# The last batch's down product in seven half-size products, with its norms taken in halves of columns

## The chip, the cores and the metric

The kernel runs on one core of one Trainium2 chip. The metric is the device time of one execution in microseconds (us); the profile's span, from the first to the last instruction, is about 1 to 2 us shorter. Engines in the profile: PE (TensorE, matrix products), PEld (its weight loads), DVE (VectorE), ACT (ScalarE), POOL (GpSimd) and SP (SyncE, which here issues nearly all DMAs). All data are float32; a float32 matmul shows as two records.

## The reference

Eight batches of 512 tokens of width 512 go through an attention block and then a feed-forward block:

```python
x = x + layernorm(attention(layernorm(x)))
x = x + layernorm(ffn(layernorm(x)))
```

The change concerns the end of the second line. In the feed-forward block

```python
x = fwht(x * SU_ug) / SCALE
x_up = x @ W_up.T * (Wscale_ug[:INTER] * SCALE)        # 512 -> 2048 features
x_gate = x @ W_gate.T * (Wscale_ug[INTER:] * SCALE)
x = silu(x_gate) * x_up
x = fwht(x * SU_dp) / SCALE
x = x @ W_down.T * (Wscale_dp * SCALE)                 # 2048 -> 512: the down product
```

the Walsh-Hadamard transform ahead of the down product is linear, so the kernel applies it to the weights once. What is left for each batch is a product of 512 tokens x 2048 features with 2048 x 512 weights, a scale for each output column (`wsdp_bc`, the column scales copied to all partitions), a normalization of each token over its 512 columns (mean, variance, no weights), and the addition of the block's input.

## The kernel before

Attention for all eight batches takes the first 930 us or so. While it runs, the transformed down weights are written to a DRAM tensor, `wdd`. Its output, the feed-forward block's input, goes to the DRAM tensors `x1d[b]`.

The feed-forward block handles the batches in pairs. Up and gate products are made by seven products in place of eight (Strassen's scheme in Winograd's form), two batches being the two halves of the columns. From the second pair on a second level of the same scheme lies inside the first (`deep`, L1113): matmuls `d` of 128x128 weights by 128x256. Their results are summed on DVE (L1133 to L1144) and POOL (L1140, L1142, L1347) into tiles `pr`; ACT applies silu (L1164), and DVE multiplies gate, up and scale into a feature tile `g` (L1160). `g` holds 128 features x 512 tokens and is the stationary operand of the down product.

The down product of batches 0 to 6 (`psy`, L1225) is spread between the `d` matmuls of later batches. For each of the 16 feature tiles, four matmuls, one for each 128 tokens, add into four PSUM banks; the weights `wd` come from DRAM into three buffers in turn (`wd_load`, L1077). Batch b's end (`finish`, L1245) multiplies the banks by the column scales on DVE (L1250), takes the statistics (`bn`, L97: bn_stats, then bn_aggr), the inverse deviation on POOL (`inverse_std`, L102: an add at L104, a power at L105), the shift on DVE (`shift_of`, L108), the normalization on ACT (L1272) and the residual's addition on POOL (L1275), and stores (L1276). The residuals `xres` are loaded two at a time.

The last batch, 7, has nothing to be spread between. Its 16 weight tiles are loaded ahead (`wd_load_last`, L1085), the first eight into two of the tiles `xb` that had held the inputs, the last eight into two tiles `wdl`. After the last `d` matmul of the kernel, `down_rows` (L1514) makes its product `psz` (L1516): 14 of the 16 matmuls of the first 128 tokens, then the 12 matmuls that batch 6 still lacks (three feature tiles by four row blocks), then the other two, and then 16 for each of the other three row blocks. `end_rows` (L1520) ends a row block while the next one is multiplied. Each of its steps is one instruction over 128 tokens x 512 columns. Only that of the fourth row block has no matmuls beside it.

This part of the program is written under a manual schedule: each engine executes its instructions in the order in which the code issues them, with semaphore waits for operands and for the reuse of buffers. So the order of the calls is the order of the queues of PE, DVE, ACT, POOL and SP. Four PSUM banks are handed out in turn by `ubank` (L978); six buffers of 128x2x512 by `pr_tile` (L997).

Of the kernel before, what the change touches and what calls it, by code (L numbers as in the profile page):

```python
# [10 lines left out]
F32 = mybir.dt.float32  # L11
BF16 = mybir.dt.bfloat16
I32 = mybir.dt.int32
AF = mybir.ActivationFunctionType
ALU = mybir.AluOpType
AX = mybir.AxisListType

P = 128
# [3 lines left out]
NT = S // P  # L22
INTER = 2048
NI = INTER // P
# [9 lines left out]
def sandwich_kernel(  # L34
# [19 lines left out]
    nc = tc.nc  # L54
# [6 lines left out]
    stat = ctx.enter_context(tc.tile_pool(name="stat", bufs=12))  # L61
# [13 lines left out]
    wsdp_bc = const.tile([P, D], F32, name="wsdp_bc")  # L75
# [21 lines left out]
    def bn(dst, src, name):  # L97
        st = stat.tile([P, 6], F32, tag="st", name=f"st_{name}")
        nc.vector.bn_stats(out=st, in_=src)
        nc.vector.bn_aggr(out=dst, in_=st)  # L100

    def inverse_std(mv, n, name):  # L102
        rs = stat.tile([P, NT], F32, tag="rs", name=f"rs_{name}")
        nc.gpsimd.tensor_add(rs[:, :n], mv[:, :n, 1], eps[:, :n])  # L104
        nc.gpsimd.tensor_tensor(rs[:, :n], rs[:, :n], nhalf[:, :n], ALU.pow)  # L105
        return rs

    def shift_of(mv, rs, n, name):  # L108

        sh = stat.tile([P, NT], F32, tag="sh", name=f"sh_{name}")  # L110
        if n == 1:
            nc.vector.tensor_scalar(sh[:, 0:1], mv[:, 0, 0:1], rs[:, 0:1], -1.0, ALU.mult, ALU.mult)
            return sh
        nc.vector.scalar_tensor_tensor(
            sh[:, :n], mv[:, :n, 0], -1.0, rs[:, :n], ALU.mult, ALU.mult
        )
        return sh
# [4 lines left out]
    NH = NI // 2  # L122
# [31 lines left out]
    rows = [(b, t) for b in range(NB) for t in range(NT)]  # L154
    room = {}
    xrow, xflat, xb = {}, {}, {}
# [63 lines left out]
    ops, home = {}, []  # L220
# [21 lines left out]
    with ExitStack() as actx:  # L242
# [474 lines left out]
        for t in range(NT):  # L717
            xn[0, t] = row.tile([P, D], F32, tag="xn", name=f"xn_0_{t}", bufs=3)
            rs, sh = norm0[t]
# [139 lines left out]
        for t in range(NG * NT):  # L859
            n, c = divmod(t, NT)  # L860
            b, i = divmod(t, NK * NT)
# [73 lines left out]
        b = NB - 1  # L935
# [24 lines left out]
        for qc in range(NT):  # L960
            y, rs, sh = ys.pop((b, qc))
# [16 lines left out]
    def ubank(name):  # L978
        return ps_u.tile([P, S], F32, tag="u", name=name)
# [8 lines left out]
    HS = S // 2  # L988
# [8 lines left out]
    def pr_tile(name):  # L997
        return fs.tile([P, 2, S], F32, tag="pr", name=name, bufs=6)
# [72 lines left out]
    def order_of(b):  # L1071
        return [f for i in range(NH) for f in ((i, i + NH) if b % 2 == 0 else (i + NH, i))]
# [10 lines left out]
    wd_last = []  # L1083
# [11 lines left out]
    wd_home = []  # L1095
# [53 lines left out]
    waiting = {b: [] for b in range(NB)}  # L1149
# [136 lines left out]
    def proceed(by=None):  # L1286
        if ends and by in (None, ends[0][0]):
            ends.pop(0)[1]()
# [3 lines left out]
    def part():  # L1292
        if not queue:
            queue.extend(down_parts())
        if queue:
            queue.pop(0)()
# [210 lines left out]
        scale(b, f, c[:, 1], c[:, 0])  # L1507


    b = NB - 1  # L1510
    blocks = [g for _, g, _, _ in waiting[b]]
    assert order_of(b) == [f for f, _, _, _ in waiting[b]]

    def down_rows(ps, t, lo, hi):  # L1514
        for n in range(lo, hi):
            nc.tensor.matmul(  # L1516
                ps, lhsT=blocks[n][:, ts(t, P)], rhs=wd_last[n], start=n == 0, stop=n == NI - 1
            )

    def end_rows(ps, t, eng):  # L1520
        y = pr_tile(f"fy_{b}_{t}")[:, 0]
        nc.vector.tensor_mul(y, ps, wsdp_bc)
        mv = stat.tile([P, NT, 2], F32, tag="mvf", name=f"mvz_{t}")
        bn(mv[:, 0, :], y, f"z{t}")
        rs = inverse_std(mv, 1, f"z{t}")
        sh = shift_of(mv, rs, 1, f"z{t}")
        nc.scalar.activation(y, y, AF.Identity, bias=sh[:, 0:1], scale=rs[:, 0:1])
        eng.tensor_add(y, rest[t], y)
        nc.sync.dma_start(out=out[b, ts(t, P), :], in_=y)

    now[0] += 2
    while queue:
        part()
    ps = ubank("psz_0")
    down_rows(ps, 0, 0, NI - 2)
    while turn_of[0] < b:
        down()
    while ends:
        proceed()
    down_rows(ps, 0, NI - 2, NI)  # L1540
    rest = []
    for t in range(NT):
        rest.append(fs.tile([P, D], F32, tag="sig", name=f"xres_{b}_{t}", bufs=4))
        nc.sync.dma_start(out=rest[t], in_=x1d[b][ts(t, P), :])
    for t in range(NT):
        if t + 1 < NT:
            following = ubank(f"psz_{t + 1}")
            down_rows(following, t + 1, 0, NI)
        end_rows(ps, t, nc.vector if t == NT - 1 else nc.gpsimd)
        ps = following  # L1550


def _rope_table():
# [61 lines left out]
```

## Time and profile before

| | us |
|---|---|
| median of three runs (2101.5 to 2102.11) | 2101.69 |
| profiled execution, device time | 2102.66 |
| profiled execution, span | 2100.9 |
| PE busy | 2076.8 (99% of the span) |
| DVE busy | 1414.4 (67%) |
| POOL busy | 1575.4 (75%) |
| ACT busy | 745.3 (35%) |

The stretch that the change touches is the last 73 us. Busy times in four parts of it, from the profile's windows (from:to, length, then busy us and instructions of PE, PEld, DVE, ACT and POOL, the granted clock as a share of full, the DMA share and GB/s):

```profile
2027.80:2039.90 12.10, 12.10 (x30) 5.40 (x29) 3.26 (x3) 0.72 (x1) 5.59 (x5) 1.00 0.75 260
2039.90:2050.10 10.20, 10.20 (x26) 4.46 (x25) 2.05 (x3) 0.00 (x0) 0.00 (x0) 1.00 0.00 0
2050.10:2093.20 43.10, 43.07 (x101) 18.80 (x99) 9.11 (x23) 5.37 (x7) 12.14 (x15) 1.00 0.25 79
2093.20:2100.90 7.70, 0.00 (x0) 0.00 (x0) 2.48 (x5) 0.81 (x1) 0.74 (x2) 0.67 0.09 35
```

The rows are batch 7's first matmuls, batch 6's last twelve, the rest of batch 7, and what follows PE's last matmul. Times in the text are on this axis, from the span's start. In a row of the timeline the columns are start, length, engine, line, operation, output<-input, shape and count, and in brackets the engine's idle time before it with what ended it.

### The profile page before, as it was taken

To read this page: it belongs to the slowest core of one execution; us is meant where nothing else is said; L and a number is where in the kernel's file an instruction comes from. 1 tells how busy PE (TensorE), PEld (TensorE's weight loads), DVE (VectorE), ACT (ScalarE), POOL (GpSimd) and SP (SyncE) were. 2 spreads that over 40 slices of the span, in tenths; PEclk is the share of its full clock that TensorE was granted. 3 is DMA by queue.
4 is the path that set the end of the run, shared out by engine and by line. 5 is a ranking of instruction groups with operands and counts; after the bars stand their busy time and mean duration, and the time that the engine had idled before them with its cause. 6 is when DMAs were issued, how large, how long until landed. Compare 5 with 4: busy or idle time off the path is not lost.

```text
span 2100.9 us, 26741 instructions
## 1 busy us (share of the span) xinstructions
PE 2076.8 (99%) x9035; PEld 1057.4 (50%) x9042; DVE 1414.4 (67%) x2356; ACT 745.3 (35%) x1199; POOL 1575.4 (75%) x1629
## 2 busy tenths in 40 slices
PE   8999999999999999999999999999999999999998
PEld 4333333333333333344444677676676766777753
DVE  5698777676767677465545866678866678656542
ACT  3554545555555545522121122222222222222211
POOL 4787979787878889645453678788888879787852
PEclk9999999999999999999999999999999999999999
DMA  3112121212121122237454444444343344444432
GB/s 122 37 31 51 42 54 49 47 51 52 46 57 46 32 66 72 70 104 221 145 166 152 146 143 148 133 138 149 130 157 131 131 137 144 138 158 136 138 112 70
DMA packets 215913, 218.12 MB, mean 104 GB/s; under 512 B 87376, under 2 KB 147920, under 8 KB 215776
## 3 DMA queue, kind: packets, MB, share of 16 engines
q1 hardware_dynamic: 215424, 215.32, 33.2%
q8 instruction: 72, 1.18, 0.2%
q0 software_dynamic: 352, 1.08, 0.1%
q14 instruction: 65, 0.53, 0.1%
HBM read 169.18 MB, written 46.92 MB: 103 GB/s over the span
## 4 chain that ended last, share of the span: by engine, by line
PE 94%; DVE 3%; issue 1%; POOL 1%; ACT 1%; DMA 0%; SPq 0%; POOLq 0%; DVEq 0%; ACTq 0%
PE d L1123 24%; PE psy L1225 18%; PE s L527 6%; PE ops L606 6%; PE ps_k L439 5%; PE ps_y L662 5%; PE t L573 5%; PE u L1106 5%; PE g L1106 4%; PE psz L1516 3%; PE t L564 3%; PE l L623 2%; PE ps_q L454 2%; PE ps_v L466 1%; PE ps_cq L407 1%; PE fxh L207 1%
## 5 line engine op out<-in xcount | busy, mean ns | idle before, releaser
L1225 PE MATMUL psy<-wd,g 128*128 128x512 f32 x896 | 448.9, 592 | 0.0
L535 DVE TENSOR_REDUCE nm<-s 128x2 f32<-128x1024 f32 x256 | 300.8, 1216 | 175.1 <-PE s L527 175.1
L1347 POOL TENSOR_TENSOR pr<-pr,pr 128x512 f32<-128x512 f32 x294 | 391.6, 1357 | 9.0
L594 POOL TENSOR_TENSOR p<-p,p 128x512 f32<-128x512 f32 x244 | 330.2, 1384 | 22.1 <-PE ops L606 22.1
L585 ACT ACTIVATE p<-t 128x1024 f32<-128x1024 f32 x256 | 251.8, 1023 | 89.0 <-PE t L573 89.0
L1123 PE MATMUL d<-xb,wq 128*128 128x256 f32 x992 | 254.2, 380 | 1.9 <-DVE inner L1139 1.4
L1123 PEld LDWEIGHTS d<-tt,wq 128*128 128x128 f32 x864 | 164.0, 190 | 144.4 <-issue 106.0
L1123 PE MATMUL d<-tt,wq 128*128 128x256 f32 x864 | 233.8, 379 | 0.2 <-DVE pr L1144 0.2
L1140 POOL TENSOR_TENSOR pr<-inner 128x256 f32<-128x256 f32 x168 | 126.0, 750 | 138.5 <-DVE inner L1139 105.9
L1123 PEld LDWEIGHTS d<-xb,wq 128*128 128x128 f32 x992 | 186.7, 190 | 62.4 <-issue 30.1
L1225 PEld LDWEIGHTS psy<-wd,g 128*128 128x128 f32 x896 | 169.7, 190 | 49.3 <-issue 29.4
L1136 ACT COPY inner<-d 128x256 f32<-128x256 f32 x168 | 62.6, 373 | 309.6 <-PE d L1123 291.5
L1132 ACT COPY inner<-d 128x256 f32<-128x256 f32 x168 | 62.6, 372 | 300.3 <-PE d L1123 193.2
L527 PE MATMUL s<-kT,qT 32*128 32x512 f32 x1024 | 153.8, 639 | 0.7 <-DVE nm L535 0.7
L573 PE MATMUL t<-qT,kT 32*128 32x512 f32 x1024 | 142.8, 598 | 0.0
L606 PE MATMUL ops<-p,v 128*32 128x512 f32 x1024 | 136.8, 605 | 0.0
L1142 POOL TENSOR_TENSOR pr<-pr,inner 128x256 f32<-128x256 f32 x168 | 136.5, 813 | 0.0
L1123 PE MATMUL d<-T,wq 128*128 128x256 f32 x496 | 127.6, 380 | 0.2
L1144 DVE TENSOR_TENSOR pr<-d,inner 128x256 f32<-128x256 f32 x168 | 70.5, 420 | 75.5 <-PE d L1123 72.9
L439 PE MATMUL ps_k<-xT,wkr_sb 128*128 128x512 f32 x256 | 118.3, 605 | 0.7 <-ACT xT L397 0.7
L662 PE MATMUL ps_y<-wo_sb,oT 128*128 128x512 f32 x256 | 115.8, 593 | 0.9 <-DVE oT L657 0.6
L1135 DVE TENSOR_TENSOR inner<-d,inner 128x256 f32<-128x256 f32 x168 | 70.5, 419 | 62.4 <-PE d L1123 62.0
(219 smaller groups left out, 3263.8 us busy)
## 6 DMA issues: line engine op xcount, KB each, us to landing
wq<-wdeep SPq DMA_DIRECT2D x168, 448.0 KB, 4.2
wd<-wdd SPq DMA_DIRECT2D x112, 256.0 KB, 2.8
wdeep<-w SPq DMA_DIRECT2D x32, 448.0 KB, 5.5
xr<-in_x SPq DMA_DIRECT2D x32, 256.0 KB, 2.8
xin<-x1d SPq DMA_DIRECT2D x32, 256.0 KB, 4.0
xres<-x1d SPq DMA_DIRECT2D x32, 256.0 KB, 3.3
out<-fy SPq DMA_DIRECT2D x32, 256.0 KB, 2.0
rec<-rd SPq DMA_DIRECT2D x124, 64.0 KB, 2.0
```

The costliest lines, as they stand in the source:

```text
L439: nc.tensor.matmul(ps, lhsT=wkr_sb[:, k, ts(g, P)], rhs=xT[b][:, k, :], start=(k == 0), stop=(k == NK - 1),)
L527: nc.tensor.matmul(sp[j // 2][:, j % 2, :], lhsT=qT[b][rows, g, ts(qc, P)], rhs=kT[b][rows, g, :], start=True, stop=True,)
L535: nc.vector.tensor_reduce(nms[n][:, qc, 2 * h : 2 * h + 2], sp[h], AX.X, ALU.max, negate=True)
L573: nc.tensor.matmul(sp[j // 2][:, j % 2, :], lhsT=kT[b][rows, g, ts(c, P)], rhs=qT[b][rows, g, :], start=False, stop=True,)
L585: nc.scalar.activation(pt[n, c, h], sp[h], AF.Exp)
L594: nc.gpsimd.tensor_add(into, into, pt[n, c, j // 2][:, j % 2, :])
L606: nc.tensor.matmul(o_ps[n][j * DH : (j + 1) * DH, :], lhsT=vv[b][:, c, ds(g * P + j * DH, DH)], rhs=pt[n, c, j // 2][:, j % 2, :], start=( ...
L662: nc.tensor.matmul(ps, lhsT=oT[b][:, k, ts(qc, P)], rhs=wo_sb[:, k, :], start=False, stop=(k == NK - 1),)
L1106: nc.tensor.matmul(ps, lhsT=w[:, SLOT[n], k, :], rhs=rhs[:, k, :], start=k == 0, stop=k == 1)
L1123: nc.tensor.matmul(ps, lhsT=w[:, INNER[m]], rhs=rhs[m], start=True, stop=True)
L1225: nc.tensor.matmul(ys_[t], lhsT=g[:, ts(t, P)], rhs=w, start=n == 0, stop=n == NI - 1)
L1347: nc.gpsimd.tensor_add(pr[n][:, h], pr[a][:, h], pr[b][:, h])
```

## The change

The last batch's down product is cut in two along features (tiles 0 to 7 and 8 to 15), tokens (0 to 255 and 256 to 511) and output columns (0 to 255 and 256 to 511), and made by seven products instead of eight. Each has 8 feature tiles x 2 row blocks = 16 matmuls of 128x128 by 128x256, summed over the features in one PSUM bank that holds both row blocks. In the order 1, 2, 5, 6, 7, 3, 4:

- The operands that are sums of features (`sums_of`) are made on POOL, 8 instructions of 128x256 each for products 5, 6, 7 and 3, and those that are sums of weights on DVE, 4 instructions of 128x512 each for products 5, 6, 7 and 4; product 4's weights are also multiplied by the column scales (8 more of 128x256). The sums for 5, 6 and 7 are issued ahead of batch 6's ending, those for 3 and 4 after it.
- Four matmuls of product 1 stand ahead of batch 6's twelve.
- The results are combined by ACT copies, DVE and POOL additions of whole banks. The column scales are applied to the combined tiles (L1625 to L1627), before product 4 in the code.
- Statistics are taken for half rows (`rows_stats`, L1619) and joined by bn_aggr. The closing steps (`close_rows`, L1629) go over half rows too: DVE multiplies by the inverse deviation and adds the residual in one instruction (L1638), ACT adds the shift (L1639), and SP stores half rows (L1640).
- Product 4 is made one row block at a time. Between its halves in the code stand the endings of row blocks 0 and 1; then DVE adds the first half to the rest (L1651), row block 2 is ended, and after the second half row block 3.

The diff:

```diff
@@ -1507,47 +1507,150 @@
         scale(b, f, c[:, 1], c[:, 0])
     b = NB - 1
-    blocks = [g for _, g, _, _ in waiting[b]]
+    block = {f: g for f, g, _, _ in waiting[b]}
     assert order_of(b) == [f for f, _, _, _ in waiting[b]]
-    def down_rows(ps, t, lo, hi):
-        for n in range(lo, hi):
-            nc.tensor.matmul(
-                ps, lhsT=blocks[n][:, ts(t, P)], rhs=wd_last[n], start=n == 0, stop=n == NI - 1
-            )
-    def end_rows(ps, t, eng):
-        y = pr_tile(f"fy_{b}_{t}")[:, 0]
-        nc.vector.tensor_mul(y, ps, wsdp_bc)
-        mv = stat.tile([P, NT, 2], F32, tag="mvf", name=f"mvz_{t}")
-        bn(mv[:, 0, :], y, f"z{t}")
-        rs = inverse_std(mv, 1, f"z{t}")
-        sh = shift_of(mv, rs, 1, f"z{t}")
-        nc.scalar.activation(y, y, AF.Identity, bias=sh[:, 0:1], scale=rs[:, 0:1])
-        eng.tensor_add(y, rest[t], y)
-        nc.sync.dma_start(out=out[b, ts(t, P), :], in_=y)
     now[0] += 2
     while queue:
         part()
-    ps = ubank("psz_0")
-    down_rows(ps, 0, 0, NI - 2)
+    def piled(t):
+        return t.rearrange("p k (h s) -> p (k h) s", h=2)
+    sum1, sum2 = piled(xb[0]), piled(xb[1])
+    ws1, ws2 = piled(home[0]), piled(home[1])
+    wl = [t.rearrange("p (i a) (c s) -> p i a c s", a=2, c=2) for t in wd_home]
+    def rows_of(f, h):
+        return block[f][:, ts(h, HS)]
+    A = {
+        1: lambda i: rows_of(i, 0), 2: lambda i: rows_of(i + NH, 0), 5: lambda i: sum1[:, i],
+        6: lambda i: sum2[:, i], 7: lambda i: rows_of(i, 1), 3: lambda i: rows_of(i + NH, 0),
+        4: lambda i: rows_of(i + NH, 1),
+    }
+    W = {
+        1: lambda i: wl[i // 2][:, i % 2, 1, 0], 2: lambda i: wl[i // 2][:, i % 2, 0, 0],
+        5: lambda i: ws1[:, i], 6: lambda i: ws2[:, i], 7: lambda i: wl[i // 2][:, i % 2, 1, 1],
+        3: lambda i: wl[i // 2][:, i % 2, 0, 1], 4: lambda i: wl[i // 2][:, i % 2, 0, 0],
+    }
+    def sums_of(n):
+        if n in (5, 6, 7, 3):
+            for i in range(NH):
+                if n == 5:
+                    nc.gpsimd.tensor_add(sum1[:, i], A[7](i), A[4](i))
+                elif n == 6:
+                    nc.gpsimd.tensor_sub(sum2[:, i], sum1[:, i], A[1](i))
+                elif n == 7:
+                    nc.gpsimd.tensor_sub(A[7](i), A[1](i), A[7](i))
+                else:
+                    nc.gpsimd.tensor_sub(A[3](i), A[2](i), sum2[:, i])
+        for j in range(NT):
+            w, two = wl[j], ts(j, 2)
+            b11, b12, b21, b22 = w[:, :, 1, 0], w[:, :, 1, 1], w[:, :, 0, 0], w[:, :, 0, 1]
+            if n == 5:
+                nc.vector.tensor_sub(ws1[:, two], b12, b11)
+            elif n == 6:
+                nc.vector.tensor_sub(ws2[:, two], b22, ws1[:, two])
+            elif n == 7:
+                nc.vector.tensor_sub(b12, b22, b12)
+            elif n == 4:
+                nc.vector.tensor_sub(b21, b21, ws2[:, two])
+                for i in range(2):
+                    nc.vector.tensor_mul(b21[:, i], b21[:, i], wsdp_bc[:, :HS])
+    acc = {}
+    def last_product(n, rows=(0, 1), lo=0, hi=NH):
+        if n not in acc:
+            acc[n] = ubank(f"psz_{n}").rearrange("p (r s) -> p r s", r=2)
+        for r in rows:
+            for i in range(lo, hi):
+                nc.tensor.matmul(
+                    acc[n][:, r], lhsT=A[n](i)[:, ts(r, P)], rhs=W[n](i), start=i == 0, stop=i == NH - 1
+                )
+    def room_for(name):
+        t = pr_tile(name)
+        return [t[:, k].rearrange("p (r s) -> p r s", r=2) for k in range(2)]
+    last_product(1, lo=0, hi=NH // 2, rows=(0,))
+    for n in (5, 6, 7):
+        sums_of(n)
     while turn_of[0] < b:
         down()
     while ends:
         proceed()
-    down_rows(ps, 0, NI - 2, NI)
+    last_product(1, lo=NH // 2, rows=(0,))
+    last_product(1, rows=(1,))
+    last_product(2)
     rest = []
     for t in range(NT):
         rest.append(fs.tile([P, D], F32, tag="sig", name=f"xres_{b}_{t}", bufs=4))
         nc.sync.dma_start(out=rest[t], in_=x1d[b][ts(t, P), :])
-    for t in range(NT):
-        if t + 1 < NT:
-            following = ubank(f"psz_{t + 1}")
-            down_rows(following, t + 1, 0, NI)
-        end_rows(ps, t, nc.vector if t == NT - 1 else nc.gpsimd)
-        ps = following
+    m1, m5 = room_for("z_m")
+    u2, u3 = room_for("z_u")
+    v, u3w = room_for("z_v")
+    y = [pr_tile(f"fy_{b}_{h}") for h in range(2)]
+    left = [t[:, :, :HS] for t in y]
+    right = [t[:, :, HS:] for t in y]
+    nc.scalar.copy(m1, acc[1])
+    nc.vector.tensor_add(left[0], acc[2], m1)
+    last_product(5)
+    nc.scalar.copy(m5, acc[5])
+    sums_of(3)
+    last_product(6)
+    nc.vector.tensor_add(u2, acc[6], m1)
+    nc.gpsimd.tensor_add(v, u2, m5)
+    sums_of(4)
+    last_product(7)
+    nc.vector.tensor_add(u3, acc[7], u2)
+    nc.gpsimd.tensor_add(right[1], u3, m5)
+    last_product(3)
+    nc.vector.tensor_add(right[0], acc[3], v)
+    stats_of = {}
+    spare = pr_tile("z_stats").rearrange("p a (t n) -> p (a t) n", t=2)
+    def rows_stats(t, part, src):
+        if t not in stats_of:
+            stats_of[t] = spare[:, t, :12].rearrange("p (h n) -> p h n", h=2)
+        nc.vector.bn_stats(out=stats_of[t][:, part], in_=src)
+    for r in range(2):
+        nc.vector.tensor_mul(u3w[:, r], u3[:, r], wsdp_bc[:, :HS])
+        nc.gpsimd.tensor_mul(right[1][:, r], right[1][:, r], wsdp_bc[:, HS:])
+        nc.vector.tensor_mul(y[0][:, r], y[0][:, r], wsdp_bc)
+    def close_rows(t):
+        h, r = divmod(t, 2)
+        mv = stat.tile([P, NT, 2], F32, tag="mvf", name=f"mvz_{t}")
+        nc.vector.bn_aggr(out=mv[:, 0, :], in_=stats_of[t])
+        rs = inverse_std(mv, 1, f"z{t}")
+        sh = shift_of(mv, rs, 1, f"z{t}")
+        for half in (left, right):
+            cols = ts(half is right, HS)
+            o = half[h][:, r]
+            nc.vector.scalar_tensor_tensor(o, o, rs[:, 0:1], rest[t][:, cols], ALU.mult, ALU.add)
+            nc.scalar.activation(o, o, AF.Identity, bias=sh[:, 0:1])
+            nc.sync.dma_start(out=out[b, ts(t, P), cols], in_=o)
+    for t in range(2):
+        rows_stats(t, 0, left[0][:, t])
+        rows_stats(t, 1, right[0][:, t])
+        rows_stats(t + 2, 1, right[1][:, t])
+    for r in range(2):
+        last_product(4, rows=(r,))
+        if r == 0:
+            close_rows(0)
+            close_rows(1)
+        nc.vector.tensor_add(left[1][:, r], acc[4][:, r], u3w[:, r])
+        rows_stats(r + 2, 0, left[1][:, r])
+        close_rows(r + 2)
 def _rope_table():
```

## The prediction

> **What bounds the kernel now.** First the page's busy shares and its chain: PE is busy 99% of the span and is 94% of the chain, so the edit is judged by where PE waits and by what is left after its last matmul. Then the chain in order of time over the end of the span (start, length, what):
>
> ```profile
> 1993.92 1.73 PE d L1123 x8
> ...
> 2027.94 12.02 PE psz L1516 x28
> 2039.96 10.30 PE psy L1225 x24
> 2050.26 42.93 PE psz L1516 x100
> ...
> 2093.21 0.70 DVE fy L1522
> ...
> 2097.21 0.69 DVE fy L1528
> ```
>
> The last batch's down product (psz) is 128 records, two per matmul, in 54.95 us, without a gap, around the 12 psy matmuls of batch 6. 128x256 matmuls (d) run at 0.216 us a record. After PE only 4.7 us of work follow to 2097.9, then the last store.
>
> Second, the timelines of DVE, GpSimd and SyncE where the last down product starts, for who delays whom:
>
> ```profile
> 2027.35 1.28 POOL L1275 TENSOR_TENSOR fy<-xres,fy 128x512 f32<-128x512 f32 x1
> 2027.46 2.85 DVE L1160 SCALAR_TENSOR_TENSOR g<-pr,wsu 128x512 f32<-128x512 f32 x2
> 2028.58 1.19 POOL L1140 TENSOR_TENSOR pr<-inner 128x256 f32<-128x256 f32 x1
> 2029.73 1.17 POOL L1142 TENSOR_TENSOR pr<-pr,inner 128x256 f32<-128x256 f32 x1
> ...
> 2032.91 0.38 SPq L1080 DMA_DIRECT2D wd<-wdd  x1
> 2033.50 0.75 DVE L1160 SCALAR_TENSOR_TENSOR g<-pr,wsu 128x512 f32<-128x512 f32 x1 [3.19 <-POOL pr L1347]
> ```
>
> An L1160 (two SBUF inputs) takes 0.75 us alone, 1.43 beside POOL; POOL's 128x256 add takes 1.18 there against a median of 0.73. They take turns: about 1.16 us for one of each. The last wd load is issued at 2032.91 behind eight wdl loads; the tile's own answer for 2030 to 2060 gives its landing:
>
> ```profile
> DMA to landing us min/median/max: 6.0/6.0/6.0
> ```
>
> so it is there at 2038.9. Third, one row block's closing steps, and the granted clock (PEclk, before DMA) around PE's last matmul:
>
> ```profile
> 2094.67 0.18 DVE L100 BATCH_NORM_AGGREGATE mvz<-st_z 128x2 f32<-128x6 f32 x1
> 2094.93 0.19 POOL L104 TENSOR_TENSOR rs_z<-mvz,eps 128x1 f32<-128x1 f32 x1 [10.48 <-DVE mvz L100]
> 2095.19 0.55 POOL L105 TENSOR_TENSOR rs_z<-rs_z,nhalf 128x1 f32<-128x1 f32 x1
> 2095.78 0.21 DVE L112 TENSOR_SCALAR sh_z<-mvz,rs_z 128x1 f32<-128x1 f32 x1 [0.93 <-POOL rs_z L105]
> ```
>
> ```profile
> 2093.20:2095.80 2.60, 0.00 (x0) 0.00 (x0) 1.59 (x4) 0.00 (x0) 0.74 (x2) 1.00 0.00 0
> 2095.90:2100.90 5.00, 0.00 (x0) 0.00 (x0) 0.78 (x2) 0.81 (x1) 0.00 (x0) 0.50 0.14 54
> ```
>
> From one aggregate to its shift are 1.11 us, through POOL. The clock was halved 2.6 us after PE fell idle.
>
> **The change part by part** (times on the profile's axis)
>
> *PE work.* 64 matmuls of 128x512 (54.95/64 = 0.859 us) become 112 of 128x256 at half that, 0.429 (the d row gives 0.433, each matmul with a weight load of its own, as here): 48.1 us, so -6.9 us. Bounds: -6.9 to -6.5.
>
> *Order at the start.* Four matmuls (1.7 us) instead of 14 now stand ahead of batch 6's 12 psy matmuls, which start at 2029.66 instead of 2039.96. The third group of four needs the last wd at 2029.66 + 8 x 0.859 = 2036.5; it lands at 2038.9: PE waits +2.4 us. Bounds: 0 (the wd load before it landed in 2.7 us) to 2.4. I take 2.4; nothing ahead of that load in SP's queue moves. Its g, from the scale at 2033.5, is there by 2034.7. The gap is a little shorter than the 2.6 us that halved the clock at the end; should it halve it too, up to 2.5 us more would be lost, which the range's upper end takes in.
>
> *POOL's and DVE's operand sums.* POOL adds 24 of 128x256 from 2033.4; DVE runs that scale and 12 subtractions of 128x512. Thirteen turns of 1.16 end at 2048.5 (the last wdl lands near 2038.2, as DVE reaches it); POOL's other 11 at 0.69 end at 2056.1. Products 5, 6 and 7 start at 2054, 2061 and 2068, so this is covered. What is late is batch 6's ending, queued behind it: DVE multiplies and norms from 2048.5 (4 x 0.61 + 3.3) to 2054.2, but POOL takes the variances only at 2056.1 (2054.3 before). From there to the fourth L1275 the trace has 2064.96 - 2054.27 = 10.7 us, with the two xres loads in it: 2066.8. Then come the eight POOL sums for product 3: two alone, six in turns with DVE's operands of product 4 at about 1.05 (between 1.16 with a 128x512 partner and, estimated, 0.95 with a 128x256 one), to 2074.5. Product 3 starts at 2075.0 and wants the eighth at 2078.0. Covered, by 3.5 us. DVE's 12 operations for product 4 (alone 5.6 us, with turns about 10 from 2068.2) end near 2078.5, wanted at 2081.9: covered. The xres loads of batch 7 go out behind batch 6's last store, near 2067, and land by 2073, wanted at 2087. ACT's two copies wait behind its four L1272, to 2061.4; their PSUM banks are wanted from 2068: cover 6 us.
>
> *End of product 3.* 2027.94 + 10.30 + 2.4 + 96 x 0.429 = 2081.85. Before it PE is the chain, after it DVE.
>
> *DVE's tail.* Back to back, 128x512 steps start 0.61 apart, 128x256 ones 0.335. C12's add and two scalings by 512 (1.83), two by 256 (0.67), six statistics of half a row at 0.335 (estimate: half the shape; 0.2 to 0.69 as bounds, from the aggregate and the whole row) make 2.0; two closings of 1.11 + 0.13 + two multiply-adds of 0.38 = 2.0 each; then the add that takes the first half of product 4 and its release of PE, 0.45. Sum 8.95: 2090.8.
>
> *The wait that the change adds.* Both halves of product 4 lie in one PSUM tile, and in the built order the second half's first matmul waits for DVE's read of the first. That read stands behind both closings. So PE, done with the first half at 2085.3, idles 5.5 us, and eight matmuls are still to come. At full clock they take 3.4 us, at half 6.9. The clock row above says that 2.6 us of idleness halved it; at the start of the trace PE's first 22 records, 5.06 us of work, ran slow (0.23 us each, 0.15 later). With 5 us at half rate, 2.5 of the 3.4 are done and 0.9 remain: 5.9, my value, nearest to a row of this trace. End: 2096.8.
>
> By the Trainium skill (TensorE: Matmul & The Clock Gate, Part 1) the gate halves the clock after an idle window of about 3.4 us and restores it after one busy window. By that estimate the eight take 5.1 to 6.9 us and the span would be 2102.6 to 2104.4; no run here has shown such a gap yet.
>
> *The last closing.* Add and statistics 0.90, 1.11, 0.13, 0.38 + 0.45 = 2.97; ACT on half a row 0.55 (between the copy's 0.37 and L1272's 0.81); the store 2.97 as before (2097.93 to 2100.9; half the bytes, not counted; the eight half stores cost SP 0.33 each and only the last is on the path): 2096.8 + 2.97 + 0.6 + 2.97 = 2103.4. Against 2100.9 that is +2.5. The profiled execution took 2102.66, so 2105.2; it stands 1.0 above the median of 2101.69, which gives **2104.2 us**. Parts: -6.9 PE work, +2.4 wd, +7.0 from the longer ending.
>
> **The rivals**
>
> *B. PE keeps or soon regains its clock.* The second half takes 3.4: -2.5, 2101.7. Against it: the clock row. Without the wd wait as well, 2099.3.
>
> *C. POOL is late for product 3 (slower).* If DVE and POOL never overlap, 24 x 0.69 + 13 x 0.5 = 23.1 us, both end at 2056.6, batch 6's ending follows that and not 2048.5, the variances come at 2062.3, the eighth sum at 2080.7: 2.7 us past 2078.0, 2106.9. It decides from variances later than 2059.6 on, one for one; past 2061.3 it is over +0.2%. For it: L1160 reached 1.72. Against: the rows above show turns.
>
> *D. The gain arrives (faster).* Were PE never held and the ending as long as now, -6.9: 2094.8. For it: 99% PE. Against it: the wait in the built order and the 19 DVE steps between product 3 and the read.
>
> **How the numbers follow.** 0.2% is 4.2 us, about what a measurement of this kernel can tell from no change: the borders are 2097.5 and 2105.9. My case A (2101.9 to 2106.5) 0.56, of which 0.06 lies over 2105.9; B 0.14; C 0.26; D 0.04, half of it beyond the border. Slower 0.32, same 0.66, faster 0.02. The range leaves out D, the lower part of B without the wd wait, and the worst of C (a POOL that is later still): 2100.5 to 2108.0.
>
> **What would show it.** PE: psy with a gap of 2.4 us before its last eight records; no gap before product 3; a gap of 5 to 6 us between the halves of product 4, released by DVE's add, then records near 0.43 us, not 0.215, and a granted clock of 0.5 there. DVE: from product 3's end eleven steps without idling, then idle only for POOL's rs_z until the second half. POOL: L1551 ending before 2078. Wrong would make it: a gap before product 3 (C), a clock of 1.0 in the last gap (B), or bn_stats of half a row near the price of a whole one (+2 us).

## The result, and the profile after

The changed kernel takes 2105.94 us (median of 17 executions, 2103.59 to 2108.91) against 2101.77 before (17, 2101.17 to 2103.73). The ratio is 1.0019, 95% interval 1.0011 to 1.0026: about 4 us slower, at the border between "no change" and "slower by 0.2%". The prediction was 2104.2 in a range of 2100.5 to 2108.0, with "within 0.2%" the likeliest.

The profiled execution of the changed kernel took 2105.73 us, span 2104.0. In it the first psz matmul starts at 2026.57, 1.2 us earlier than in the profile before (2027.78), so the spans are compared from there: 73.1 us to the end before, 77.4 after, +4.3, which is what the medians say.

PE's timeline over the changed stretch:

```profile
2026.57 1.89 PE L1573 MATMUL psz<-xb,g 128*128 128x256 f32 x8
2028.30 7.03 PE L1225 MATMUL psy<-wd,g 128*128 128x512 f32 x16
2037.32 5.37 PE L1225 MATMUL psy<-wd,g 128*128 128x512 f32 x8 [1.99 <-DMA wd<-wdd]
...
2054.61 13.98 PE L1573 MATMUL psz<-T,xb 128*128 128x256 f32 x64
...
2083.96 1.89 PE L1573 MATMUL psz<-wdl,g 128*128 128x256 f32 x8
2091.53 3.78 PE L1573 MATMUL psz<-xb,g 128*128 128x256 f32 x8 [5.67 <-DVE fy L1651]
2095.10 2.23 PE L1573 MATMUL psz<-wdl,g 128*128 128x256 f32 x8
```

PE has two gaps, and they are the two that were forecast: 1.99 us for the last wd load, and 5.67 us between product 4's halves, ended by DVE's read of the first half (L1651). Ahead of products 5, 6, 7 and 3 there is none. But the eight psy records behind the first gap take 5.37 us, where eight should take half of the 7.03 that the sixteen before them took, and the sixteen psz records behind the second take 5.8, where sixteen take 3.6 elsewhere (two rows of 1.89, which overlap by 0.16). The windows over these places (columns as in the table before; the granted clock stands before the DMA share) show why:

```profile
2034.34:2037.76 3.42, 1.43 (x4) 0.46 (x3) 3.42 (x4) 0.00 (x0) 3.42 (x4) 1.00 0.95 362
2037.76:2041.17 3.41, 3.41 (x5) 1.33 (x4) 3.41 (x4) 0.00 (x0) 3.41 (x4) 0.50 0.01 5
2041.17:2044.58 3.41, 3.41 (x14) 2.39 (x13) 3.41 (x4) 0.00 (x0) 3.41 (x4) 1.00 0.00 0
2088.96:2092.37 3.41, 0.84 (x2) 0.75 (x3) 2.21 (x8) 1.57 (x4) 0.86 (x3) 0.50 0.28 96
2092.37:2095.78 3.41, 3.41 (x9) 2.69 (x9) 1.00 (x3) 0.91 (x2) 0.63 (x2) 0.50 0.32 105
2095.78:2099.19 3.41, 1.55 (x7) 1.02 (x6) 1.06 (x3) 0.00 (x0) 0.53 (x2) 1.00 0.09 29
```

The clock is halved for 3.41 us after the first gap and for 6.83 us around the second half of product 4. The rows are cut at the points at which the clock changes.

The operand sums and batch 6's ending, on POOL:

```profile
2032.21 8.63 POOL L1545 TENSOR_TENSOR xb<-g,g 128x256 f32<-128x256 f32 x8
2040.81 8.21 POOL L1547 TENSOR_TENSOR xb<-xb,g 128x256 f32<-128x256 f32 x8
2048.98 5.52 POOL L1549 TENSOR_TENSOR g<-g 128x256 f32<-128x256 f32 x8
2054.46 0.20 POOL L104 TENSOR_TENSOR rs_o<-mvo,eps 128x4 f32<-128x4 f32 x1
...
2065.98 6.33 POOL L1551 TENSOR_TENSOR g<-g,xb 128x256 f32<-128x256 f32 x8
```

The first sums take 1.08 us each beside DVE's, the eight of L1549 0.69 alone. The sums for product 3 end at 2072.3; product 3 starts at 2075.3.

The end, from the chain of waits:

```profile
2082.51 0.69 DVE fy L1615
...
2085.07 1.96 DVE z_stats L1622 x6
2087.03 0.12 DVE mvz L1632
...
2089.08 0.13 DVE mvz L1632
...
2091.14 0.34 DVE fy L1651
2091.53 5.82 PE psz L1573 x16
2097.37 0.43 DVE fy L1651
...
2100.07 0.51 ACT fy L1639
```

From product 3's end at 2082.5, DVE needs 9.0 us to the read that lets PE go on; then PE is the chain for 5.8 us, then DVE, POOL and ACT to the last store.

The bill, from the first psz matmul to the end, counted from start to start of the records (which makes each gap 0.16 us longer than the idle time): PE's matmuls 112 x 0.432 = 48.4 instead of 54.95 us, -6.6; the gap for the load +2.1; the halved clock behind it 5.2 (to 2042.52) instead of 3.4, +1.8; the gap in product 4 +5.8; the halved clock behind it +2.2; after PE's last matmul 6.7 instead of 7.7 us, -1.0. Sum +4.3.

### The profile page after: what moved, and what is told of

The parts are those of the page before. It is cut to its first block, busy times and chain, and to the rows that moved or that the text cites. A ratio compares the mean times of both kernels' runs of the same rounds, so it can differ in the third digit from the quotient of the medians.

```text
span 2104.0 us, 27052 instructions
## 1 busy us (share of the span) xinstructions
PE 2074.9 (99%) x9138; PEld 1077.6 (51%) x9138; DVE 1441.7 (69%) x2397; ACT 746.2 (35%) x1205; POOL 1603.9 (76%) x1662
## 3 DMA queue, kind: packets, MB, share of 16 engines
q0 software_dynamic: 352, 1.08, 0.1%
## 4 chain that ended last, share of the span: by engine, by line
PE 93%; DVE 4%; POOL 1%; issue 1%; ACT 1%; DMA 0%; SPq 0%; DVEq 0%; POOLq 0%; ACTq 0%
PE d L1123 23%; PE psy L1225 18%; PE s L527 6%; PE ops L606 6%; PE ps_k L439 5%; PE ps_y L662 5%; PE t L573 5%; PE u L1106 5%; PE g L1106 4%; PE t L564 3%; PE psz L1573 2%; PE l L623 2%; PE ps_q L454 2%; PE ps_v L466 1%; PE ps_cq L407 1%; PE fxh L207 1%
```

## The experiments

The theory: two waits of PE, and the clock that each of them costs, take more than the 6.6 us that the scheme saves. Rivals: the end is set by DVE's own steps with PE's wait beside them; POOL's sums are late; the second half of product 4 is slow for another reason than the clock. The first four kernels ran together (before: 2101.69, 33 executions), the other three in a second group (before: 2102.05, 16 executions). "Less" and "more" below are differences of medians from the changed kernel's 2105.94 us (before: 2101.77), so they carry what the medians of the kernel before differ by, up to 0.4 us; the ratios are free of that.

**Product 4's halves in two banks**

```diff
-        if n not in acc:
-            acc[n] = ubank(f"psz_{n}").rearrange("p (r s) -> p r s", r=2)
+        if n not in acc or rows == (1,) and n == 4:
+            acc[n] = ubank(f"psz_{n}_{rows[0]}").rearrange("p (r s) -> p r s", r=2)
...
+        halves.append(acc[4])
-        nc.vector.tensor_add(left[1][:, r], acc[4][:, r], u3w[:, r])
+        nc.vector.tensor_add(left[1][:, r], halves[r][:, r], u3w[:, r])
```

> Product 4's second half goes into a PSUM bank of its own, so that its first matmul no longer waits for DVE's read of the first half. Theory (the read in the same tile holds PE for 5.7 us and that idleness halves the clock): no gap between the halves, the second half's 16 records at 0.216 us, end near 2089.3 on the changed kernel's axis; DVE reads it when its third closing is done, near 2094.05 instead of 2097.37: 3.3 us less, 2102.6 us. Rival (the end is set by DVE's own steps and the wait lies beside them): within 0.5 us of 2105.9. The gap of 2 us in the psy matmuls and its clock stay.

Measured: 2103.11 us (11 executions), 2.8 less; ratio to before 1.0003 [0.9994, 1.0012]. The second half follows the first without a gap, and DVE's second add comes 3.0 us behind the first instead of 6.3:

```profile
2086.41 1.89 PE L1573 MATMUL psz<-xb,g 128*128 128x256 f32 x8
2088.14 1.89 PE L1573 MATMUL psz<-wdl,g 128*128 128x256 f32 x8
```

```profile
2091.88 0.34 DVE fy L1653
...
2094.85 0.35 DVE fy L1653
```

So the wait was on the path for some 3 of its 8 us (gap and slow records together); the rest lay beside DVE's closing of row block 2. The rival that it is hidden falls.

**The wd load ahead of the eight wdl loads.** The loop that issues the psy parts still queued, and with the last of them this load, moves up:

```diff
+    while queue:
+        part()
     for _ in range(8):
         wd_load_last()
...
     now[0] += 2
-    while queue:
-        part()
```

> The load of the last wd tile is issued ahead of the eight wdl loads; PE's order is unchanged. Theory: it lands near 2030.8, PE's gap of 2.0 us before the last four psy matmuls goes, and with it the clock that it halves in some executions (1.75 us in the profiled one): 2.0 to 3.75 us less, 2102.2 to 2103.9 us; the gap between product 4's halves stays at 5.7 us. Rival (the later wdl tiles hold DVE's operands, or POOL is late now that product 3 starts 3.7 us earlier): a gap of 1 us or more ahead of product 5 or 3, and 2105 us or more.

Measured: 2102.62 us (11), 3.3 less; ratio 1.0005 [0.9996, 1.0014]. The 24 psy records run without a gap, and the gap in product 4 is as it was:

```profile
2030.26 10.46 PE L1225 MATMUL psy<-wd,g 128*128 128x512 f32 x24
...
2089.57 3.78 PE L1573 MATMUL psz<-xb,g 128*128 128x256 f32 x8 [5.68 <-DVE fy L1651]
```

Some 2.0 of the 3.3 us are the wait. The other 1.3 are a remainder, put down to the clock behind the wait; the interval of the ratio is wide enough (1.9 us either way) that the runs do not fix this share. That the clock is halved in some executions only is shown: four profiles have this gap, and the eight records behind it take 5.37 us in two of them and 3.67 us in the other two. Between the profiles the early load saves 3.6 us (73.9 us from the first psz matmul to the end instead of 77.4), although the second half of product 4 took 6.3 us there instead of 5.8. No other gap opens.

**PE kept busy in product 4's gap**

```diff
         last_product(4, rows=(r,))
         if r == 0:
+            idle = ubank("psz_idle")
+            for k in range(12):
+                nc.tensor.matmul(
+                    idle[:, :HS], lhsT=A[2](k % NH)[:, :P], rhs=W[3](k % NH), start=True, stop=True
+                )
```

> Twelve matmuls of 128x256 into a spare PSUM bank that nothing reads are put between product 4's halves, so that PE works while it would wait; the wait itself stays. Theory (the second half is slow only because the clock was halved): the second half takes 3.45 us instead of 5.8, 2.4 us less, 2103.5 us, and the granted clock is 1.0 there. Rival (it is slow for a reason of its own, such as the bank that DVE has just read): it stays at 5.8 us and the time within 0.5 us of 2105.9.

Measured: 2103.2 us (11), 2.7 less; ratio 1.0007 [0.9998, 1.0016]. The wait is still there, now 0.51 us behind the idle work, and the sixteen records take 3.7 us at a granted clock of 1.00:

```profile
2037.54 3.67 PE L1225 MATMUL psy<-wd,g 128*128 128x512 f32 x8 [2.19 <-DMA wd<-wdd]
...
2090.07 1.99 PE L1573 MATMUL psz<-xb,g 128*128 128x256 f32 x8 [0.51 <-DVE fy L1656]
2091.90 1.89 PE L1573 MATMUL psz<-wdl,g 128*128 128x256 f32 x8
```

Twelve matmuls whose results nothing reads make the kernel faster. The wait, the bank and the read by DVE are as they were, so the sixteen records had been slow for the clock. The first line shows something more: a gap of 2.19 us ahead of psy, and the clock was not halved behind it (3.67 us).

**Both repairs**

> Product 4's halves in two banks and the wd load first. Theory: PE has no gap of over 1 us from the first psz matmul to the last, the clock stays at 1.0, and both gains add: 5.3 to 7.1 us less than the changed kernel, 2098.9 to 2100.6 us, 0.05 to 0.14% under the kernel before; single executions spread by about 1 us instead of 5. Rival (POOL's or DVE's operands come next): a gap ahead of product 3 takes back 1 us or more and the time is over 2101 us.

Measured: 2099.35 us (11, 2098.12 to 2101.01); ratio 0.9987 [0.9978, 0.9996], 2.3 us under the kernel before. PE has no gap and the clock stays at 1.0 to its end. The times add as forecast. The spread did not shrink as forecast: 2.9 us, and the kernel before spread by 3.2 in the same group, so most of the spread is not from this place.

**The endings overlapped.** On top of both repairs, the four closings change places. `deviations` makes bn_aggr and the inverse deviations, for row blocks 0 and 1 in one pass through POOL; `take` is DVE's add of one half of product 4 with its statistics and bn_aggr; the other steps are as in the changed kernel:

```diff
...
+    first_two = deviations((0, 1))
+    third = take(0)
+    close_rows((0, 1), *first_two)
+    fourth = take(1)
+    close_rows((2,), *third)
+    close_rows((3,), *fourth)
```

> On top of the two banks and the early wd load: DVE takes the first half of product 4 and its statistics while POOL makes the inverse deviations of row blocks 0 and 1 (both in one pass), and the second half before it closes row block 2. Theory (after product 3 the end is DVE's chain with four idle trips through POOL of 0.94 us each, of which three can be covered): about 3.8 us less between the end of product 3 and the last store than with the two edits alone, 2095.5 us, 0.3% under the kernel before. Rival (another step sets the end: ACT's eight shifts, SP's eight stores, or PE): less than 1.5 us gained.

Measured: 2095.02 us (6 executions); ratio 0.9969 [0.9958, 0.9981], 0.3% faster than the kernel before. After product 3, its DVE idles only once for POOL by more than 0.1 us:

```profile
2085.34 0.18 DVE L114 SCALAR_TENSOR_TENSOR sh_z<-mvz,rs_z 128x2 f32<-128x2 f32 x1
2085.44 1.66 DVE L1642 SCALAR_TENSOR_TENSOR fy<-fy,rs_z,xres 128x256 f32<-128x256 f32 x4
2087.03 0.41 DVE L1647 TENSOR_TENSOR fy<-psz,z_v 128x256 f32<-128x256 f32 x1
...
2089.45 0.21 DVE L112 TENSOR_SCALAR sh_z<-mvz,rs_z 128x1 f32<-128x1 f32 x1 [0.45 <-POOL rs_z L105]
```

From product 3's end (2079.54) to the last closing step's start (2089.58) are 10.0 us; with the two repairs alone they are 13.7 (2078.73 to 2092.45).

**POOL made late.** The changed kernel with

```diff
                 else:
+                    if i == 0:
+                        for k in range(12):
+                            nc.gpsimd.tensor_sub(sum1[:, k % NH], A[1](k % NH), sum2[:, k % NH])
                     nc.gpsimd.tensor_sub(A[3](i), A[2](i), sum2[:, i])
```

> The changed kernel with 12 more POOL subtractions of 128x256 ahead of its sums for product 3 (they write into a tile that is no longer read). In the profile the eighth of those sums ends at 2072.3 and is wanted at 2078.3, so POOL has 6.0 us to spare. Theory (POOL is covered, up to that point): the 12 take 8.5 to 9.5 us, PE waits 2.5 to 3.5 us ahead of product 3's last matmuls, and the time grows by that, and by up to 1.7 us more where the clock is halved: 2108.4 to 2111 us. Rival (POOL is already what product 3 waits for): 8.5 us or more, 2114 us and over.

Measured: 2111.8 us (5, 2109.41 to 2112.28), 5.9 more than the changed kernel, a little over the range given and far from the rival's. The 12 took 10.7 us, 0.89 each beside DVE. PE waited 3.94 us ahead of product 3, released by its first sum, and then made the first part of the product at half clock, and the whole in 10.0 us from its first record to DVE's step behind it instead of 7.2:

```profile
2066.93 10.69 POOL L1553 TENSOR_TENSOR xb<-g,xb 128x256 f32<-128x256 f32 x12
2077.58 6.31 POOL L1554 TENSOR_TENSOR g<-g,xb 128x256 f32<-128x256 f32 x8
```

```profile
2072.97 1.89 PE L1576 MATMUL psz<-wdl,g 128*128 128x256 f32 x8
2078.80 3.81 PE L1576 MATMUL psz<-xb,g 128*128 128x256 f32 x8 [3.94 <-POOL g L1554]
2082.41 2.85 PE L1576 MATMUL psz<-wdl,g 128*128 128x256 f32 x8
```

The slack is real: of 10.7 us of POOL work, product 3 ended only 6.9 later (4.1 from start to start, and 2.8), so some 4 were covered. The forecast had 6.0, from a profile in which product 3 itself came 1.8 us late by the halved clock behind the first gap; in this execution that clock was not halved (the psy records behind the gap took 3.67 us), and PE wanted the sums earlier. Most of the rest of the miss is the 12 subtractions, longer than expected. The 2.8 us are not the clock alone. POOL's eighth sum ends at 2083.89 (2077.58 + 6.31), 5.1 us after the product's first record; at full clock its matmul would have stood 3.0 us after that record (seven of 0.432). So at any clock some 2.1 of the 2.8 us would have gone to POOL's pace, and by these rows the halved clock added about 0.7.

**The closing in halves alone**, in the kernel before, for its fourth row block:

```diff
...
+        for half in range(2):
+            cols = ts(half, HS)
+            o = y[:, cols]
+            nc.vector.scalar_tensor_tensor(o, o, rs[:, 0:1], rest[t][:, cols], ALU.mult, ALU.add)
+            nc.scalar.activation(o, o, AF.Identity, bias=sh[:, 0:1])
+            nc.sync.dma_start(out=out[b, ts(t, P), cols], in_=o)
```

> The kernel before, with only its fourth row block's closing as in the changed kernel: the multiply-add with the residual on DVE and the shift on ACT, in halves of columns, stored in halves; its statistics stay whole. Theory: from the shift to the last store's issue 1.5 us instead of 2.15, 0.6 us less, 2101.1 us, which the times hardly tell. Rival (two half steps cost as much as one whole on each engine, and the second store queues): no shorter, or longer, in the profile.

Measured: 2101.64 us (11); ratio 0.9998 [0.9989, 1.0007], no difference that the times can tell. In the profile ACT starts its first half only at the second half's DVE step's end, so little overlaps:

```profile
2095.54 0.21 DVE L112 TENSOR_SCALAR sh_z<-mvz,rs_z 128x1 f32<-128x1 f32 x1 [0.93 <-POOL rs_z L105]
2095.67 0.87 DVE L1535 SCALAR_TENSOR_TENSOR fy<-fy,rs_z,xres 128x256 f32<-128x256 f32 x2
2096.52 0.91 ACT L1536 ACTIVATE fy<-fy,sh_z 128x256 f32<-128x256 f32 x2 [13.65 <-DVE fy L1535]
```

From the shift's start to ACT's end are 1.9 us; before, from the shift to the last addition's end, 2.1. Expected were 1.5. In the changed kernel itself the same steps take that long, 1.55 us from the shift's start to ACT's end, because there ACT starts after DVE's first half step:

```profile
2099.43 0.21 DVE L112 TENSOR_SCALAR sh_z<-mvz,rs_z 128x1 f32<-128x1 f32 x1 [0.93 <-POOL rs_z L105]
2099.56 0.87 DVE L1638 SCALAR_TENSOR_TENSOR fy<-fy,rs_z,xres 128x256 f32<-128x256 f32 x2
```

```profile
2100.07 0.91 ACT L1639 ACTIVATE fy<-fy,sh_z 128x256 f32<-128x256 f32 x2 [5.35 <-DVE fy L1638]
```

So the halves overlap in one kernel and hardly in the other; why ACT starts later in the kernel before with this closing is not shown.

## Why the prediction was right, point by point

- *PE's work*, -6.9 predicted: -6.6. A 128x256 matmul took 0.432 us, the d row's price, not half of the 128x512 one. It came near the other bound, -6.5.
- *The wait for the last wd*, +2.4: 2.0 idle. The load landed 5.5 us after its issue instead of 6.0. With the load issued ahead of the eight others it landed in 2.7 us and the gap was gone: the wait is the order of the loads.
- *The clock behind that wait.* This is the step that was mis-sized. The prediction named it ("should it halve it too, up to 2.5 us more would be lost") but put nothing into the sum. It cost 1.8 us in the profiled execution and, as the remainder of the early load's gain, about 1.3 over the executions. With it the sum of +2.5 would have been +3.8 to +4.3; measured are 4.2 by the medians and 4.3 by the profiles. That nothing else is missing is partly luck: the terms for PE's work and for the wait were each off by 0.3 us, in opposite directions.
- *POOL's and DVE's sums covered*: right. They ended 3.0 us ahead of product 3's start and took turns as the rows before had shown (1.14 us for a pair, 1.16 predicted). The slack, forecast as 3.5 us, was 6.0 in the profile (2072.3 against 2078.3) and about 4 where the clock behind the first gap is not halved, as the late POOL shows. It shrinks as PE's waits go: with both repairs the eight sums run from 2065.28 to 2072.88 and product 3 starts at 2071.55, so the eighth, wanted at 2074.6, has 1.7 us to spare.
- *End of product 3 to PE's release*, 8.95 us: 9.0, in the profile from 2082.51 to 2091.53. The half-row statistics took 0.33 each.
- *The wait between the halves*, 5.5 us idle and 5.9 for the second half: 5.67 and 5.8. Two banks remove it; idle work in the gap removes its clock part. The mechanism was right; that 5.9 came so close is partly luck. It rests on 5 us at half clock, and in this profile 4.25 us of the second half were (2091.53 to 2095.78); it took 6.3 us in the profile with the early load and 5.5 in that with POOL late. All three lie within the 5.1 to 6.9 us of the prediction's second estimate. The last section shows what the difference goes with.
- *The last closing*, 2.97 + 0.6 + 2.97: in the profile 6.6 from the second add to the end.
- *Rival B* (the clock stays) is what the idle work made: 2.7 us less. *Rival C* (POOL late) did not occur; when it was made to, the eighth sum came 6.2 us past its time (2083.89 against 2077.7: without the wait product 3 would have started at 2074.7, and its eighth matmul stands 3.0 us behind its first) and product 3 ended 6.9 late: its price of one for one, and about 0.7 for the clock. *Rival D* (the gain arrives) needed the repairs: even with both waits gone the kernel gained only 2.3 us of the 6.6, because the ending after product 3 had become DVE's, with four trips through POOL. Covering three of them gave another 4.3 by the medians, of two groups, and 3.7 in the profiles.

## What to carry to other kernels

Fewer matmuls help only if PE has no new wait: look at the built order for what the first matmul of each group waits for, a load queued behind others and a reader of the same PSUM bank above all: here two halves in one bank tied the second half's start to the first half's read, and two banks freed it. Price a PE gap of 2 us or more at the gap plus what a halved clock may take of the matmuls behind it (here 1.8 to 2.7 us where it was halved, nothing in two of the four profiles with the gap of 2 us). Where the last engine's chain goes through another engine for one small value per row block, let it take the next block's work while it waits. And check the cover of the other engines again after each repair: here POOL's fell from 6.0 to 1.7 us.

## What the runs showed of the hardware

In all nine profiles the clock changes at distances that are whole multiples of 3.41 us (in the changed kernel at 2037.76, 2041.17, 2088.96 and 2095.78: 1, 14 and 2 of them). What the halving goes with is PE's idle time within one such stretch, not the length of a gap. In the part of the program that the change touches, stretches with 1.99, 2.48 and 2.67 us of idleness were followed by a halved clock, those with 1.41 and 1.82 us were not, although the gaps there were 2.19 and 2.22 us long: they lay across two stretches. Over the whole of the nine profiles no stretch at full clock with 1.86 us of idleness or less was followed by a halved clock, but for the one named below, and every one with 1.99 us or more was. Shown for the kernel with two banks and for the one with idle work (after the stretch come its length and PE's busy time; the clock stands ahead of the DMA share):

```profile
2035.56:2038.97 3.41, 0.93 (x2) 0.49 (x3) 3.20 (x4) 0.00 (x0) 3.41 (x4) 1.00 0.73 279
2038.97:2042.38 3.41, 3.41 (x5) 1.32 (x4) 3.41 (x4) 0.00 (x0) 3.41 (x4) 0.50 0.00 0
```

```profile
2033.35:2036.76 3.41, 2.00 (x5) 0.57 (x3) 3.41 (x4) 0.00 (x0) 3.41 (x4) 1.00 1.01 360
2036.76:2040.17 3.41, 2.63 (x6) 1.25 (x7) 3.33 (x4) 0.00 (x0) 3.41 (x4) 1.00 0.25 94
```

So the same gap costs a halved clock in one execution and none in the next. The Trainium skill (TensorE: Matmul & The Clock Gate, Part 1) has the free-running stretch of this length, and halves the clock after one that is idle; here one that was 58% idle (1.99 of 3.41) was enough. Idle time is not the whole measure: in the profile with the early load, a stretch of the attention part with 0.74 us idle, most of it in matmuls of 32 rows, was followed by a halved clock too, and in the other eight it was not. Why is open. On the way back, at half clock, stretches with 1.28, 1.66 and 2.57 us of idleness did not restore it and full ones did.
